# Attention of layer 0: runs of nine scores over seven one-bank PSUM tiles in place of runs of seven over tiles of three, two and two banks

## Chip, core and metric

The kernel runs on one core of a Trainium2 chip. The metric is the device time of one launch in microseconds (us). TensorE (PE) multiplies matrices into PSUM, which has eight banks of 512 float32 values on each of 128 partitions; ScalarE (ACT) computes exponentials and copies, VectorE (DVE) adds, GpSimd (POOL) and SyncE (SP) issue DMAs. Each engine works through its own queue in order and waits on semaphores for the others.

## The reference

Two layers on a tensor `x` of shape (2, 256, 64, 64), each of them `x + layer(groupnorm(x))`. Only layer 0 is touched by the change:

```python
qkv = jnp.einsum('bchw,oc->bohw', x, qkv_w) + qkv_b[None, :, None, None]
qkv = qkv.reshape(b, 3, num_heads, head_dim, n)        # 8 heads of 32, n = 4096
q, k, v = (qkv[:, 0], qkv[:, 1], qkv[:, 2])
attn_logits = jnp.einsum('bhci,bhcj->bhij', q, k) * scale
attn_weights = jax.nn.softmax(attn_logits, axis=-1)
out = jnp.einsum('bhij,bhcj->bhci', attn_weights, v)
```

So for each of 2 x 8 heads a 4096 x 4096 matrix of scores is made, its exponentials are multiplied by `v`, and the result is divided by the sums of the exponentials. Layer 1 (local attention in blocks, 1x1 convolutions and a depthwise convolution) follows for each of the two batch entries.

## The kernel before

The program does, for each of the two batch entries in turn, the projections of layer 0, `attention0`, and layer 1. `attention0` cuts the work of one entry into 16 groups `g` (8 heads, two halves of the queries), each group into 32 blocks `j` of 128 keys (`NJ`), and each block into 4 units `u` of 512 queries (`T`). A unit is a 128 x 512 tile of scores; an entry has 2048 units, the program 4096.

A unit goes through these steps:

- **Score** (L505, in `scores`): one matmul of 128 x 512 into one PSUM bank.
- **Exponential** (L511): ACT reads the scores from PSUM and writes the values to SBUF, into a ring of 28 places of 512 columns (`RING`; 17 places lie in the tile `es`, the other 11 in the tile that the profile names `v`).
- **Value product** (`quarters`, L521): four matmuls of 32 columns each, one per unit of the block, side by side on TensorE, into the bank `av`. Blocks 1 to 30 of a group are done in two halves of 256 columns (`work_of` yields between them), blocks 0 and 31 in one piece of 512. One `next(work)` is one such step, 62 for a group.
- **Sums**: for most blocks DVE adds the values of the block to running sums `e` (L558, `add_rows`); for the blocks in `SUMMED` POOL issues DMAs that add in memory to `acc` (L566, L568, `add_in_memory`).

At the end of a group ACT copies the product out (L762), the sums are multiplied by a matrix of ones into a spare PSUM bank (`sum_rows`, the same L521), and ACT copies these (L598, `finish`).

The order on PE, ACT and DVE is the order in which the program is written (`manual_schedule`). The loop at the end of `attention0` alternates two parts, which together are called a pass below: `scores` puts out up to seven scores with their exponentials, and then steps of earlier units are taken from `steps()`. `scores` uses three PSUM tiles: `sa` of three banks, `sb` and `sc` of two; one exponential reads a whole tile. `have` is the number of units that were scored before this pass, so the value products lie behind the seven scores just issued. Steps are taken while fewer than `share` are done, while the ring needs places (`must`), in the last pass, or while a bank is asked for:

```python
while begun < ready and (taken < share or begun < must or final or use is not None):
```

When something wants a PSUM bank (`wanted`: the sums of a group, a few statistics), `scores` leaves the third bank of `sa` unused in that pass, hands it out, and the pass has six scores. PSUM is full: 3 + 2 + 2 banks for scores, one for `av`.

Of the kernel before, what the change touches and what calls it, by code (L numbers as in the profile page):

```python
# [9 lines left out]
F32 = mybir.dt.float32  # L10
I32 = mybir.dt.int32
F32R = mybir.dt.float32r
AF = mybir.ActivationFunctionType
# [4 lines left out]
P = 128  # L18
B, C, H, W = 2, 256, 64, 64
N = H * W  # L20
T = 512
# [4 lines left out]
NH0 = C // HD0  # L26
# [14 lines left out]
def direct_layers(ctx: ExitStack, tc: tile.TileContext, a: dict, out: bass.AP, bad: bass.AP):  # L41
# [3 lines left out]
    nc = tc.nc  # L45
# [11 lines left out]
    psum = {}  # L57

    def w4(shape, name, dtype=F32):
        return work.tile(shape, dtype, tag="w4", name=name)  # L60
# [304 lines left out]
    SC0 = 1.0 / math.sqrt(HD0)  # L365
# [8 lines left out]
    NJ = N // P  # L374
# [77 lines left out]
    RING, RING_A = 28, 17  # L452
# [11 lines left out]
    def attention0(b, xts, held):  # L464
# [10 lines left out]
        n_units = NH0 * 2 * NJ * 4  # L475
# [4 lines left out]
        places = []  # L480
        n_places = 0

        def at_places(first, n):

            while n > 0:
                at = first % RING
                m = min(n, (RING_A if at < RING_A else RING) - at)
                yield m, es[:, at : at + m, :] if at < RING_A else held["es"][:, at - RING_A : at - RING_A + m, :]
                first, n = first + m, n - m

        def scores(spare):

            nonlocal n_places
            bank = None
            for tag, size in (("sa", 3), ("sb", 2), ("sc", 2)):
                first = len(places)
                n = min(size - (spare and size == 3), n_units - first)
                if n <= 0:
                    break
                sc = psum["sc"].tile([P, size, T], F32, tag=tag, name=f"{tag}_{b}_{first}")  # L500
                if spare and size == 3:
                    bank = sc[:, size - 1, :]
                for i in range(n):
                    g, (j, u) = (first + i) // (4 * NJ), divmod((first + i) % (4 * NJ), 4)
                    nc.tensor.matmul(  # L505
                        sc[:, i, :], held["k", g // 2][:, j * P : (j + 1) * P], held["q", g, u // 2][:, u % 2, :],
                        start=True, stop=True,
                    )
                i = 0
                for m, dst in at_places(n_places, n):  # L510
                    nc.scalar.activation(dst, sc[:, i : i + m, :], AF.Exp, scale=SC0)  # L511
                    i += m
                places.extend(range(n_places, n_places + n))
                n_places += size
            return bank

        def quarters(dst, lhs, rhs, start, stop, part=None):

# [17 lines left out]
        def add_rows(g, j):  # L536
            if j == 0:
                sums[g] = psum["sc"].tile([P, T], F32, tag="av", name=f"av_{b}_{g}")
                added[g] = [w4([P, 2, T], f"e_{b}_{g}_{w}") for w in range(2)]
                return  # L540
            for w in range(2):
                dst = added[g][w]
                if j in summed(g):
                    if w == 0:
                        add_in_memory(g, j)
                    continue
                if j == 1:
                    first = two_units(g, 0, w), two_units(g, 1, w)
                    if len(first[0]) == len(first[1]) == 1:
                        nc.vector.tensor_add(dst, first[0][0][1], first[1][0][1])  # L550
                    else:
                        for s in range(2):
                            nc.vector.tensor_add(dst[:, s, :], unit(g, 0, 2 * w + s), unit(g, 1, 2 * w + s))
                    continue
                for s, src in two_units(g, j, w):
                    if g == last and j in SUMMED_LAST:
                        continue
                    nc.vector.tensor_add(dst[:, s, :], dst[:, s, :], src)  # L558
# [11 lines left out]
        def work_of(g, j):  # L570


            if (g, j) < (last, NJ - 3):
                add_rows(g, j)
            for part in (None,) if j in (0, NJ - 1) else range(2):
                if part == 1:
                    yield
                quarters(
                    sums[g], held["v"][:, (g // 2) % 2, j, :], lambda u: unit(g, j, u), j == 0, j == NJ - 1, part
                )  # L580

        def sum_rows(g, rows):
            if g == last:
                for part in range(2):
                    for j in SUMMED_LAST:
                        quarters(rows, ones, lambda u: unit(g, j, u), j == SUMMED_LAST[0], False, part)
                    quarters(rows, ones, lambda u: acc[u], False, False, part)
                    quarters(rows, ones, lambda u: added[g][u // 2][:, u % 2, :], False, True, part)
                return
            quarters(rows, ones, lambda u: added[g][u // 2][:, u % 2, :], True, True)  # L590
# [140 lines left out]
        def steps():  # L731

            for done in range(NH0 * 2 * NJ):
                g, j = divmod(done, NJ)
                if (g, j) == (last, NJ - 3):
                    assert len(places) == n_units
                    held["rows"] = psum["sc"].tile([P, 3, T], F32, tag="sa", name=f"rows_{b}")[:, 2, :]
                    for i in (NJ - 3, NJ - 2, NJ - 1):
                        add_rows(g, i)
                    sum_rows(g, held["rows"])  # L740
                for _ in work_of(g, j):
                    yield done
                if g and j == 0:

                    for w in range(2):
                        dst = added[g - 1][w]
                        for s in range(2) if w == 0 else (slice(0, 2),):
                            nc.vector.tensor_add(dst[:, s, :], dst[:, s, :], acc[s] if w == 0 else pair)
                    waiting.clear()
                if g and j == 1:  # L750
                    wanted.append(late[0].send)
                if g and j in (9, 17):
                    next(late[0])
                for what in also.get((g, j), ()):
                    what()
                if j == 4 and g % 2 == 0 and g // 2 + 1 < NH0:
                    fetch_head(b, g // 2 + 1, held)
                if j == NJ - 1:
                    waiting.append(g)
                    avs = w4([P, 2, T], f"avs_{b}_{g}")  # L760
                    if g < last:
                        nc.scalar.copy(avs[:, 0, :], sums[g])  # L762
                    copied[g] = avs
                    late[:] = [finish(g)]
                    next(late[0])
                    if g + 2 < NH0 * 2:
                        fetch_queries(b, g + 2, held)
                yield done + 1

        E = mybir.EngineType  # L770
        with tc.manual_schedule(engines={E.PE, E.Activation, E.DVE}):

            per_group = 2 * NJ - 2
            work, begun, taken = steps(), 0, 0
            scores(False)
            final = False
            while not final:
                have = len(places)  # L780
                use = wanted.pop(0) if wanted else None
                bank = scores(use is not None)
                final = have == n_units
                ready = have // 4
                share = have * per_group // (4 * NJ) - 2

                must = sum(place < n_places + 7 - RING for place in places[: 4 * ready : 4])
                if must % NJ == 1:
                    must += 1
                assert must <= ready  # L790
                here = 0
                while begun < ready and (taken < share or begun < must or final or use is not None):
                    if use is not None and here == 2:
                        use(bank)
                        use = None
                        continue
                    here += 1
                    group = begun // NJ
                    begun = next(work)
                    taken += 1  # L800
                    if begun // NJ > group and begun >= must and not final and use is None:
                        break
                if use is not None:
                    use(bank)
            assert next(work, None) is None
            return *finish_last(last), st
# [585 lines left out]
    for b in range(B):  # L1392
        xts = x_first if b == 0 else ahead["xts"]
        w0 = w0_first if b == 0 else ahead["w0"]
        with tc.tile_pool(name=f"ps0_{b}", bufs=8, space=PSUM) as psum["ps"]:
# [7 lines left out]
            held = project0(b, xn, w0)  # L1403
# [571 lines left out]
```

## Time and profile before

| what | us |
|---|---|
| three timed runs | 3116.66, 3120.94, 3121.48 |
| median of them | 3120.94 |
| profiled execution, first to last instruction (its span) | 3116.4 |
| attention of the first entry, first score to last product | 118.4 to 1161.1 |
| attention of the second entry | 1666.3 to 2709.4 |
| the rest (projections, layer 1, weights) | about 1030 |

Of the profiled execution only the span is given; the shortest timed run is 0.3 us longer than it, the median 4.5 us. A row of the profile's groups reads: line, engine, operation, what is written <- what is read, shapes, number of instructions | time in which at least one of them ran (us), mean duration of one (ns) | idle time of the engine before them (us) and whose work ended it. Durations of neighbours on one engine overlap, so the rate of an engine is read from the distance of two starts, not from a duration. PEld is TensorE's loading of weights, which runs beside its products.

### The profile page before, as it was taken

To read this page: it belongs to the slowest core of one execution; us is meant where nothing else is said; L and a number is where in the kernel's file an instruction comes from. 1 tells how busy PE (TensorE), PEld (TensorE's weight loads), DVE (VectorE), ACT (ScalarE), POOL (GpSimd) and SP (SyncE) were. 2 spreads that over 40 slices of the span, in tenths; PEclk is the share of its full clock that TensorE was granted. 3 is DMA by queue.
4 is the path that set the end of the run, shared out by engine and by line. 5 is a ranking of instruction groups with operands and counts; after the bars stand their busy time and mean duration, and the time that the engine had idled before them with its cause. 6 is when DMAs were issued, how large, how long until landed. Compare 5 with 4: busy or idle time off the path is not lost. (4 is left out here: it accounts for less than half of the span.)

```text
span 3116.4 us, 62659 instructions
## 1 busy us (share of the span) xinstructions
PE 3031.2 (97%) x25129; PEld 1830.6 (59%) x25129; DVE 2467.0 (79%) x3126; ACT 2313.6 (74%) x2436; POOL 836.7 (27%) x923
## 2 busy tenths in 40 slices
PE   6999999999999999999989999999999999999998
PEld 4555555555555556677755555555555555476765
DVE  4599989999899999856556998989989999834543
ACT  2699999999999984622237999999999999734333
POOL 2022222222222231055301222222222222305440
PEclk9999999999999999999999999999999999999999
DMA  7969679797897761230159687796888975700000
GB/s 241 270 132 185 143 150 172 154 178 150 164 181 154 145 133 33 75 134 29 41 193 268 128 176 151 156 176 138 177 162 164 181 153 123 170 4 4 21 14 22
DMA packets 243787, 424.41 MB, mean 136 GB/s; under 512 B 99112, under 2 KB 109916, under 8 KB 241308
## 3 DMA queue, kind: packets, MB, share of 16 engines
q0 software_dynamic: 94992, 238.36, 39.8%
q1 hardware_dynamic: 147580, 181.68, 21.6%
q8 instruction: 199, 3.26, 0.4%
q14 instruction: 104, 0.85, 0.1%
q10 hardware_dynamic: 912, 0.27, 0.0%
HBM read 119.03 MB, written 68.39 MB: 60 GB/s over the span
## 5 line engine op out<-in xcount | busy, mean ns | idle before, releaser
L558 DVE TENSOR_TENSOR e<-e,es 128x1024 f32<-128x1024 f32 (+1 forms) x956 | 1038.6, 1142 | 79.6 <-ACT es L511 77.9
L521 PE MATMUL av<-es,v 128*32 128x256 f32 (+1 forms) x9644 | 746.7, 390 | 0.0
L558 DVE TENSOR_TENSOR e<-e,v 128x1024 f32<-128x1024 f32 (+1 forms) x640 | 675.2, 1107 | 47.7 <-ACT v L511 46.6
L511 ACT ACTIVATE es<-sa 128x1536 f32<-128x1536 f32 (+1 forms) x444 | 635.7, 1432 | 93.1 <-PE sa L505 54.9
L505 PE MATMUL sa<-q,k 128*128 128x512 f32 x1736 | 561.4, 430 | 9.2 <-ACT avs L598 3.5
L521 PE MATMUL av<-v 128*32 128x256 f32 (+1 forms) x6228 | 506.5, 389 | 0.0
L521 PEld LDWEIGHTS av<-es,v 128*32 128x32 f32 x9644 | 316.1, 109 | 299.4 <-issue 160.6
L505 PEld LDWEIGHTS sa<-q,k 128*128 128x128 f32 x1736 | 280.0, 188 | 291.8 <-issue 135.4
L505 PE MATMUL sc<-q,k 128*128 128x512 f32 x1180 | 371.4, 396 | 1.7 <-ACT es L511 0.7
L505 PE MATMUL sb<-q,k 128*128 128x512 f32 x1180 | 371.0, 395 | 1.1 <-ACT es L511 1.1
L521 PEld LDWEIGHTS av<-v 128*32 128x32 f32 x6228 | 216.5, 109 | 178.6 <-issue 81.2
L511 ACT ACTIVATE es<-sc 128x1024 f32<-128x1024 f32 x296 | 306.9, 1037 | 0.0
L511 ACT ACTIVATE v<-sc 128x1024 f32<-128x1024 f32 x294 | 304.9, 1037 | 0.1
L511 ACT ACTIVATE es<-sb 128x1024 f32<-128x1024 f32 x296 | 302.0, 1020 | 3.8 <-DMA acc<-es 3.8
L511 ACT ACTIVATE v<-sb 128x1024 f32<-128x1024 f32 x294 | 300.0, 1020 | 0.0
L505 PEld LDWEIGHTS sb<-q,k 128*128 128x128 f32 x1180 | 221.2, 188 | 55.4 <-ACT es L511 2.9
L505 PEld LDWEIGHTS sc<-q,k 128*128 128x128 f32 x1180 | 210.5, 188 | 71.8 <-ACT es L511 12.1
L511 ACT ACTIVATE v<-sa 128x1536 f32<-128x1536 f32 (+1 forms) x146 | 209.2, 1433 | 35.6 <-PE sa L505 17.0
L948 PE MATMUL mm<-v,wf 128*128 128x256 f32 x1024 | 227.6, 380 | 1.5 <-DVE z L957 1.5
L568 POOL DMA_DIRECT2D es<-es x116 | 98.9, 853 | 475.6 <-ACT es L511 424.3
L948 PEld LDWEIGHTS mm<-v,wf 128*128 128x128 f32 x1024 | 193.3, 190 | 36.8 <-issue 9.9
L938 POOL TENSOR_TENSOR v<-col 128x512 f32<-128x512 f32 x128 | 165.1, 1316 | 179.2 <-ACT rk_sr L1089 39.2
(262 smaller groups left out, 3179.0 us busy)
## 6 DMA issues: line engine op xcount, KB each, us to landing
acc<-es POOLq DMA_DIRECT2D x128, 512.0 KB, 6.2
acc<-v POOLq DMA_DIRECT2D x84, 512.0 KB, 6.4
es<-es POOLq DMA_DIRECT2D x136, 256.0 KB, 4.5
v<-es POOLq DMA_DIRECT2D x132, 256.0 KB, 5.1
k<-wk_halves SPq DMA_DIRECT2D x64, 512.0 KB
q<-wq_halves SPq DMA_DIRECT2D x256, 128.0 KB
v<-v POOLq DMA_DIRECT2D x90, 256.0 KB, 5.4
es<-v POOLq DMA_DIRECT2D x86, 256.0 KB, 3.9
```

The lines of the kernel that those rows point to most:

```text
L505: nc.tensor.matmul(sc[:, i, :], held["k", g // 2][:, j * P : (j + 1) * P], held["q", g, u // 2][:, u % 2, :], start=True, stop=True,)
L511: nc.scalar.activation(dst, sc[:, i : i + m, :], AF.Exp, scale=SC0)
L521: nc.tensor.matmul(dst[HD0 * u : HD0 * u + HD0, n], lhs, rhs(u)[:, n], start=start, stop=stop)
L558: nc.vector.tensor_add(dst[:, s, :], dst[:, s, :], src)
L568: nc.gpsimd.dma_start(out=dst, in_=src, accum_op=ALU.add)
L938: (nc.gpsimd.tensor_add if plus else nc.gpsimd.tensor_sub)(dst, rows(one), rows(two))
L948: nc.tensor.matmul(mm[:, m, r, :], wf[:, k, 4 * r + q, m * P : (m + 1) * P], v[r // 2][:, r % 2, k, :], start=k == 0, stop=k == KC - 1,)
```

## The change

It replaces the three score tiles by seven tiles of one bank, `s0` to `s6`, which are used in rotation (`next_bank`), each unit with its own exponential. A run has nine scores (`PHASE`) instead of seven, so the eighth and ninth score of a run use the banks of its first and second. Value products are taken up to `behind` = 7 units behind the units scored so far, this run included. A bank that is asked for is the next in the rotation after the run, and the run keeps its nine scores. The condition for taking steps gains `ending` (the last two steps of a group), and the last three blocks are left for the last pass.

```diff
-        def scores(spare):
+        BANKS, PHASE = 7, 9
+
+        def next_bank():
 
             nonlocal n_places
-            bank = None
-            for tag, size in (("sa", 3), ("sb", 2), ("sc", 2)):
-                first = len(places)
-                n = min(size - (spare and size == 3), n_units - first)
-                if n <= 0:
-                    break
-                sc = psum["sc"].tile([P, size, T], F32, tag=tag, name=f"{tag}_{b}_{first}")
-                if spare and size == 3:
-                    bank = sc[:, size - 1, :]
-                for i in range(n):
-                    g, (j, u) = (first + i) // (4 * NJ), divmod((first + i) % (4 * NJ), 4)
-                    nc.tensor.matmul(
-                        sc[:, i, :], held["k", g // 2][:, j * P : (j + 1) * P], held["q", g, u // 2][:, u % 2, :],
-                        start=True, stop=True,
-                    )
-                i = 0
-                for m, dst in at_places(n_places, n):
-                    nc.scalar.activation(dst, sc[:, i : i + m, :], AF.Exp, scale=SC0)
-                    i += m
-                places.extend(range(n_places, n_places + n))
-                n_places += size
-            return bank
+            at = n_places
+            n_places += 1
+            return at, psum["sc"].tile([P, T], F32, tag=f"s{at % BANKS}", name=f"s_{b}_{at}")
+
+        def scores():
+
+            for unit in range(len(places), min(len(places) + PHASE, n_units)):
+                g, (j, u) = unit // (4 * NJ), divmod(unit % (4 * NJ), 4)
+                at, sc = next_bank()
+                nc.tensor.matmul(
+                    sc, held["k", g // 2][:, j * P : (j + 1) * P], held["q", g, u // 2][:, u % 2, :],
+                    start=True, stop=True,
+                )
+                ((_, dst),) = at_places(at, 1)
+                nc.scalar.activation(dst[:, 0, :], sc, AF.Exp, scale=SC0)
+                places.append(at)
...
-                    held["rows"] = psum["sc"].tile([P, 3, T], F32, tag="sa", name=f"rows_{b}")[:, 2, :]
+                    held["rows"] = next_bank()[1]
...
+            behind, reach = 7, PHASE + 1
             work, begun, taken = steps(), 0, 0
-            scores(False)
-            final = False
-            while not final:
-                have = len(places)
+            while begun < NH0 * 2 * NJ:
+                scores()
                 use = wanted.pop(0) if wanted else None
-                bank = scores(use is not None)
-                final = have == n_units
-                ready = have // 4
+                bank = next_bank()[1] if use is not None else None
+                final = len(places) == n_units
+                have = n_units if final else len(places) - behind
+                ready = max(0, have) // 4
                 share = have * per_group // (4 * NJ) - 2
 
-                must = sum(place < n_places + 7 - RING for place in places[: 4 * ready : 4])
+                must = sum(place < n_places + reach - RING for place in places[: 4 * ready : 4])
...
-                while begun < ready and (taken < share or begun < must or final or use is not None):
+                while begun < ready:
                     if use is not None and here == 2:
                         use(bank)
                         use = None
                         continue
+                    ending = taken % per_group >= per_group - 2
+                    if not (taken < share or ending or begun < must or final or use is not None):
+                        break
+                    if not final and begun == NH0 * 2 * NJ - 3:
+                        break
```

## The prediction

> **What bounds the kernel now.** The change touches only the attention stretches, so I first ask the busy time of the engines in the first of them (118 to 1164 us of the span), then the order of time on TensorE inside it, then that on ScalarE.
>
> ```profile
> core 0: us, PE busy (x) PEld busy (x) DVE busy (x) ACT busy (x) POOL busy (x), PEclk, DMA share, GB/s
> 118.00:1164.00 1046.00, 1039.25 (x10192) 591.28 (x10192) 958.29 (x980) 974.80 (x926) 279.27 (x340) 1.00 0.80 161
> ```
>
> PE is busy in 99%, but ACT (93%) and DVE (92%) are not far behind, and the clock is fully granted. A PE that is never idle can still lose time between products of different kinds, which only the starts show. The timeline of PE over one pass (start, duration, instructions):
>
> ```profile
> 606.18 0.96 PE L505 MATMUL sa<-q,k 128*128 128x512 f32 x3
> 606.98 0.63 PE L505 MATMUL sb<-q,k 128*128 128x512 f32 x2
> 607.45 0.63 PE L505 MATMUL sc<-q,k 128*128 128x512 f32 x2
> 608.00 1.50 PE L521 MATMUL av<-es,v 128*32 128x256 f32 x24
> 609.43 0.96 PE L505 MATMUL sa<-q,k 128*128 128x512 f32 x3
> ```
>
> From start to start the pass takes 3.25 us: 1.82 for seven scores, 1.43 for 24 records of products (8 records are one step of 256 columns). Inside a run two scores start 0.231 us apart, inside the products 8 records take 0.432 (0.054 each). At that rate the pass would take 7 x 0.231 + 3 x 0.432 = 2.91. The rest, 0.337, is paid at the changes of kind: the second score starts 0.337 after the first (0.106 too late), the first product 0.326 after the last score (0.095 too late), and the products' 1.432 hold 0.136 more than 3 x 0.432. The starts of all 588 runs in the trace (294 passes an entry) give the same numbers: medians 0.337, 0.231 and 0.327.
>
> So the two attention stretches can be added up from PE alone: 588 runs x 0.337 = 198; 4096 scores x 0.231 = 946; 15872 records at 0.054, those of blocks 0 and 31 doubled, = 885; the sums of 30 groups, 0.864 each, = 26. Together 2055, and the passes add up to 23 more (5.6 of them at the two starts). PE sets the pace nearly everywhere, and 198 us of its time are changes of kind. Now ACT, its timeline over the end of a group, and, in a second fence, rows of its groups by shape:
>
> ```profile
> 639.64 1.01 ACT L511 ACTIVATE es<-sb 128x1024 f32<-128x1024 f32 x1
> 640.54 1.03 ACT L511 ACTIVATE es<-sc 128x1024 f32<-128x1024 f32 x1
> 641.44 0.61 ACT L762 COPY avs<-av 128x512 f32<-128x512 f32 x1
> 641.92 1.49 ACT L511 ACTIVATE es<-sa 128x1536 f32<-128x1536 f32 x1
> 643.27 1.05 ACT L511 ACTIVATE es<-sb 128x1024 f32<-128x1024 f32 x1
> ```
>
> ```profile
> L1132 ACT ACTIVATE y<-py 128x512 f32<-128x512 f32 x32 | 19.1, 597 | 49.6 <-PE py L1128 48.1 <-PE at_lr L1058 1.5
> L762 ACT COPY avs<-av 128x512 f32<-128x512 f32 x30 | 18.2, 606 | 0.0
> L598 ACT COPY avs<-sa 128x512 f32<-128x512 f32 x30 | 17.6, 586 | 0.1
> ```
>
> Starts lie closer than durations: 0.90 us after a 1024-wide exponential (median 0.901), 1.35 after a 1536-wide one (1.349), 0.46 to 0.48 after the 512-wide copy (0.463 where no later wait shows). Seven units cost ACT 1.349 + 0.901 + 0.904 = 3.15 us, under the pass's 3.25 to 3.69.
>
> **The change, part by part.**
>
> *Fewer runs on PE.* In the order of instructions of the changed kernel the runs of scores are 454 in place of 588; the number of scores and of value products is the same. 134 x 0.337 = 45.1 us less. That is all on the path, since PE sets the pace. A pass that hands out a bank no longer shrinks to six scores, which is in this count.
>
> *An exponential per bank.* 1770 exponentials become 4096 of 512 columns. No row shows a 512-wide exponential behind another, so its price p, from start to start, is bounded by neighbours. Lower end: a line through 1.349 and 0.901 gives 0.453. Higher: a `sa` of two banks (in passes that hand out the third) is 0.922 from start to start, one of three 1.349, so a bank of 512 columns costs 0.427 and the first exponential of a pass has 0.069 fixed. An `sb`, next in the stream, keeps 0.901 - 0.854 = 0.047, say 0.048. The copy keeps 0.463 - 0.427 = 0.036, and it is 0.011 shorter than an activation of its size (586 against 597). With 0.048, p = 0.475; with 0.069, 0.496. I take 0.475, the price of a stream of activations, and keep 0.453 to 0.496.
>
> [...]
>
> ACT's need at my price: 4096 x 0.475 = 1946, and 60 copies x 0.463 = 28, together 1974. PE's is 2055 - 45 = 2010. ACT has 36 us of slack, 1.1 us for each of 32 groups, where today it has 2055 - (588 passes x 3.15 + 28) = 175. This is the narrow place of the change. Every ns on p is 4.1 us of ACT; the two needs meet at p = 0.484, and ACT alone takes the 2078 of today at p = 0.500. With the waits on both sides I put the point of no gain at 0.492 to 0.496.
>
> *New waits in the run.* Each score waits for the exponential that read its bank seven scores earlier, the eighth and ninth for the first two of their own run. Behind them on PE are all the products. When PE leaves a run, at most seven exponentials are open, 3.3 us of ACT, and products of four steps with the changes of kind take 2.2. So at the next run up to 1.1 us are open, the first new exponential ends at about 1.7 (0.6 more), and the eighth score is due at 1.72, the ninth at 1.95 against 2.2 for its bank. A pass of four steps (9 x 0.231 + 0.337 + 1.728 = 4.14) is shorter than nine exponentials (4.28), one of five (4.58) longer; the order of the changed kernel goes 4, 5, 4, 4, 5, the mean with the groups' ends 2010 / 454 = 4.43. The late ninth score costs at most 0.13 in half of the runs, 30 us, and nothing where the five-step pass has paid ahead; banks hold 1.1 us of lead, so I take 5 us, ends 0 and 30. The products themselves wait for nothing new: the ninth score has waited for the exponential seven behind, the last that they read.
>
> *The ends of groups.* The copies L762 and L598 stand behind the open exponentials as today. The sums now wait for the exponential that read the third bank of the run, long done after two steps. Today's 17 us of stalls outside the starts, mostly 0.3 to 0.4 at such places, stay; with less ACT slack they could be 0 to 10 us more, which I put into the 30 above.
>
> *Sums, DMAs, ring.* DVE's adds are 1336 of 1024 columns against 1332, and 232 against 236 halves: nothing. Its 958 us busy (durations, whose neighbours overlap by 0.08) fit into 1046 - 22 = 1024 with 94%. It runs behind ACT and holds ring places only; ACT shows no wait for it now. The queues of POOL and SP have the same DMAs in the same order but for pairs split at the ring's edge; ACT waits for them 2.3 us an entry now, and a place comes round after 28 x 0.49 = 13.8 us in place of 14.1, while they land in 4 to 6.4. Nothing, with 5 us as the other end.
>
> *Sum.* -45.1 + 5 = -40. The span of 3116.4 becomes 3076; the median of the timed runs lies 4.5 over that span, so 3120.9 - 40 = 3081.
>
> **Rivals.**
>
> ACT eats part of it: p between 0.485 and 0.492. Then ACT is the bound in the four-step passes, and -25 to -5 remain: 3096 to 3116. For it speaks how close the two needs are, 36 us in 2010; against it the 0.048 that no size of stream exceeds.
>
> ACT becomes the bound, and the kernel is slower: p over 0.496, which decides the sign. The mechanism is one: 2326 more activations, each with its own fixed part and its own wait for PE and for DVE or a DMA, whose order ACT has to take one at a time. From 0.500 on each 10 ns cost some 37 us: 0.510 gives 3185. For it: only the copy shows such a width in a stream, and a fixed part after a wait is 0.069, reached if ACT, now often just ahead of PE, starts cold each time. Against it: an ACT that waits has time to spare, so cold starts fall where they cost little.
>
> The change does not speed anything, because DVE, at 94%, becomes late with ring places and PE falls back to today's pace: about 3120. For it: the groups near the end have 5 us of statistics more. Against it: ACT waits for DVE nowhere now.
>
> **How the numbers follow.** Forecast -40: 0.66. Partial gain: 0.10, of which 0.07 over the bound. Slower by ACT: 0.19. DVE: 0.05, half of it no change and half slower. A measurement of this kernel can tell 0.2%, 6.2 us, from no change. Faster: 0.66 + 0.07 = 0.73; same: 0.03 + 0.025 = 0.055, taken as 0.06; slower: 0.21. The forecast's own range is 3070 (p = 0.453, no new stall, and today's stalls shortened by 6) to 3098 (p at 0.482 or stalls of 20). For 8 in 10 the upper end takes in the partial gain and the slower side up to p = 0.496, 15 us over today: 3136. Left out are p of 0.5 and more, about 0.16, and 0.03 below.
>
> **What would show it.** In the profile after: 454 runs of nine, each change of kind still 0.337 in sum; PE at 99% of an attention of about 1023 us an entry; exponentials of 512 columns 0.47 to 0.48 from start to start where none waits; ACT about 97% busy. Wrong are these steps if scores wait for ACT by more than 30 us in sum, if starts are over 0.49 apart in a stream (then ACT shows no idle time and PE idles ahead of the eighth and ninth score), or if ACT waits for DVE or a DMA.

## The result: no change, 3119.6 us

Twelve timed runs of the changed kernel have a median of 3119.57 us, twelve of the kernel before on the same chip 3117.85. The ratio is 1.0001 with a 95% interval of 0.9993 to 1.0009: the gain of 40 us that was forecast is not there. The profiled execution of the changed kernel took 3119.5 us, 1.8 more than its span.

The busy time in the first attention stretch, the same view as before the change:

```profile
core 0: us, PE busy (x) PEld busy (x) DVE busy (x) ACT busy (x) POOL busy (x), PEclk, DMA share, GB/s
118.00:1164.00 1046.00, 1041.85 (x10202) 610.12 (x10200) 952.52 (x978) 1028.36 (x2090) 280.58 (x340) 1.00 0.80 162
```

PE still reads 99.6%, but ACT went from 975 us to 1028, 98%. PE's busy time can't show short waits here: a score's record lasts 0.395 us in the median and the next one starts 0.231 behind it, and in this trace no score that came less than 0.2 us late behind another one has idle time ahead of it. ScalarE's timeline over the end of a group (start, time from the first start to the last end, number of instructions in the row):

```profile
631.77 0.61 ACT L510 ACTIVATE es<-s 128x512 f32<-128x512 f32 x1
632.27 5.50 ACT L510 ACTIVATE v<-s 128x512 f32<-128x512 f32 x11
637.51 3.20 ACT L510 ACTIVATE es<-s 128x512 f32<-128x512 f32 x6
640.62 0.59 ACT L758 COPY avs<-av 128x512 f32<-128x512 f32 x1
641.11 5.56 ACT L510 ACTIVATE es<-s 128x512 f32<-128x512 f32 x11
```

Read by starts, eleven exponentials take 637.51 - 632.27 = 5.24 us, 0.476 each, the price that was forecast. Read by ends they take longer. The first row ends at 632.38, the second at 637.77: 5.39 us for eleven, 0.490 each. The third ends at 640.71: 2.94 for six, again 0.490. Over both attention stretches the distance of two neighbouring ends has the median 0.490 and lies between 0.481 (first percentile) and 0.494 (95th). Starts and ends drift apart: a stream begins with exponentials of 0.60 us, and each lasts some 13 ns longer than the one ahead, up to 0.9 and more. Where the durations fall back, the ends keep their distance: the exponential that starts at 604.61 lasts 0.812, the next starts 0.702 behind it and lasts 0.601, and ends 0.491 behind it. So a start is recorded here before the one ahead has ended (631.77 + 0.61 = 632.38 against 632.27 in the rows above), and the ends give the pace of the work. So the page's mean duration is no price either:

```profile
L510 ACT ACTIVATE es<-s 128x512 f32<-128x512 f32 x2500 | 1264.0, 730 | 8.3 <-PE s L505 7.1
L510 ACT ACTIVATE v<-s 128x512 f32<-128x512 f32 x1596 | 824.3, 737 | 10.7 <-PE s L505 7.1
```

From first to last exponential the two entries take 2069 us by ends. 4096 exponentials and the copies between them at 0.490 are 2037 of it, and only 33 us are gaps (places where the next end comes over 20 ns late). ScalarE is the bound.

What PE pays for it shows in its loading of weights, over two runs of nine:

```profile
604.78 1.91 PEld L505 LDWEIGHTS s<-q,k 128*128 128x128 f32 x9 [0.41 <-ACT es L510]
607.04 1.45 PEld L517 LDWEIGHTS av<-es,v 128*32 128x32 f32 x32 [0.35 <-issue]
608.90 1.68 PEld L505 LDWEIGHTS s<-q,k 128*128 128x128 f32 x8 [0.41 <-ACT v L510]
610.87 0.19 PEld L505 LDWEIGHTS s<-q,k 128*128 128x128 f32 x1 [0.28 <-ACT es L510]
611.29 0.11 PEld L517 LDWEIGHTS av<-es,v 128*32 128x32 f32 x2 [0.24 <-issue]
```

In the first run all nine weights load in a row and the products begin 2.26 us after the first load. In the second the ninth load waits for an exponential and the products begin after 2.39. The wait for the bank stands on the weight load (4086 of the 4096 loads of scores carry one), and a held load starts 0.05 us after the exponential has ended (median 0.052 in the 143 runs whose ninth score is over 20 ns late). A load that is in time starts 0.22 us ahead of its score, beside the score ahead; a late one starts with its score (0.002 us ahead), and then the first product follows that score by 0.431 us instead of 0.326. So a bank that is free when its score is due is too late here: the load of the last score was held in 258 of 450 runs, the score itself was late in only 143, and in the other 115 the first product still came 0.432 us after it.

Summed as in the prediction, the passes are 66 us longer than their rates, against 23 before; this sum is called PE's excess below. Of the 66, late eighth and ninth scores are 27 and products that come late behind a held load 25. 454 runs in place of 588 save 45, the added waits take 43.

### The profile page after: what moved, and what is told of

It is laid out like the page before. It is cut to its first block, busy times and chain, and to the rows that moved or that the text cites. A ratio compares the mean times of both kernels' runs of the same rounds, so it can differ in the third digit from the quotient of the medians.

```text
span 3117.7 us, 65724 instructions
## 1 busy us (share of the span) xinstructions
PE 3037.0 (97%) x25129; PEld 1867.5 (60%) x25129; DVE 2457.3 (79%) x3122; ACT 2420.4 (78%) x4762; POOL 838.3 (27%) x923
## 5 line engine op out<-in xcount | busy, mean ns | idle before, releaser
L510 ACT ACTIVATE es<-s 128x512 f32<-128x512 f32 x2500 | 1264.0, 730 | 8.3 <-PE s L505 7.1
L505 PE MATMUL s<-q,k 128*128 128x512 f32 x4096 | 1126.5, 413 | 7.0 <-ACT v L510 3.6
L505 PEld LDWEIGHTS s<-q,k 128*128 128x128 f32 x4096 | 732.8, 188 | 436.8 <-ACT es L510 186.7
L510 ACT ACTIVATE v<-s 128x512 f32<-128x512 f32 x1596 | 824.3, 737 | 10.7 <-PE s L505 7.1
L564 POOL DMA_DIRECT2D acc<-es x118 | 116.2, 995 | 114.8 <-ACT es L510 64.5
L564 POOL DMA_DIRECT2D es<-v x72 | 61.3, 852 | 310.0 <-ACT v L510 308.3
L955 DVE TENSOR_TENSOR z<-z,mm 128x512 f32<-128x512 f32 x32 | 22.0, 687 | 139.0 <-ACT z L954 138.6
L564 POOL DMA_DIRECT2D v<-es x112 | 124.4, 1111 | 18.0 <-ACT es L510 13.6
L564 POOL DMA_DIRECT2D acc<-v x78 | 75.2, 964 | 67.8 <-ACT es L510 30.7
L564 POOL DMA_DIRECT2D v<-v x78 | 85.9, 1101 | 12.3 <-ACT v L510 7.5
```

The costliest lines, as they stand in the source:

```text
L505: nc.tensor.matmul(sc, held["k", g // 2][:, j * P : (j + 1) * P], held["q", g, u // 2][:, u % 2, :], start=True, stop=True,)
L510: nc.scalar.activation(dst[:, 0, :], sc, AF.Exp, scale=SC0)
L564: nc.gpsimd.dma_start(out=dst, in_=src, accum_op=ALU.add)
L955: nc.vector.tensor_add(z[:, 0], z[:, 1], mm[:, :, 0, :])
```

## Experiments

Theory A: the change moved the bound to ScalarE, since an exponential has a fixed part of 0.063 us (0.490 less 0.427 for its 512 columns, the cost of one more bank in the kernel before, which is 0.834 ns a column and 0.833 in an expectation below) whatever its width, and 2326 more of them cost what PE saves. Theory B: what costs is the reuse of two banks within a run, whatever ScalarE's rate. All ratios are to the kernel before, run on the same chip.

**Runs of eight.**

```diff
-        BANKS, PHASE = 7, 9
+        BANKS, PHASE = 7, 8
```

> The changed kernel with runs of eight scores in place of nine (510 runs instead of 454), all else as changed. Theory A, ScalarE is the bound: in the changed kernel's trace exponentials of 512 columns end 0.490 us apart, so ScalarE needs 4096 x 0.490 = 2007 us and 29 more for the copies, 2036 in all, whatever the length of a run; PE needs 2010 + 56 x 0.337 = 2029. So the time stays within 10 us of the changed kernel, 3110 to 3120, and exponentials still end 0.490 apart. Theory B, the reuse of two banks inside one run is what costs (waits of the eighth and ninth score and their weight loads, about 50 us): of these more than half go, 19 us of changes of kind come back, so some 25 us are gained, 3092 to 3098.

Measured 3100.32 us, 0.9942 (0.9928 to 0.9955): faster than both kernels. Exponentials still end 0.490 apart, and ScalarE's gaps fall from 33 to 15 us; PE's excess falls from 66 to 29. The gain of 17 us lies between the two expectations. ScalarE's need of 2037 is a floor that all three lengths of run share; how near a kernel comes to it depends on the gaps, which A had left out. In the changed kernel 32 of the 33 us lie in or right behind passes of five and more steps of products; with runs of eight 13 of the 15 are waits of the copies at the ends of groups.

**Runs of seven, an exponential per bank alone.**

```diff
-        BANKS, PHASE = 7, 9
+        BANKS, PHASE = 7, 7
```

> The changed kernel with runs of seven: one exponential per bank alone, no longer runs (584 of them, no bank used twice in a run). Theory A: PE needs 2010 + 130 x 0.337 = 2054 and ScalarE 2036, so PE is the bound again by a little: within 8 us of the kernel before, 3112 to 3126, scores wait for banks under 15 us in sum. Theory B: the same time as before, without any wait for a bank. Theory C, the separate wait of every score holds up its weight load and costs PE about 0.1 us at many scores, whatever the run: clearly slower, 3145 or more.

Measured 3101.70, 0.9951 (0.9937 to 0.9965). All three expectations miss it. With nearly the old number of runs (584 against 588) it is 16 us faster than before, because PE's excess falls from 23 to 7. C is refuted: with a wait at each score PE's excess is 7 us in all 584 runs together. Of the 23 us before, 8 lay in the passes that lend a bank, 6 at the two starts and 10 in others (rounded); with runs of seven 2, 3 and 2 are left of them. Whether the gain comes from banks that are released and lent one by one or from the new order of the loop, which came with them, was not separated.

**Exponentials of 448 columns in the changed kernel.**

```diff
-                nc.scalar.activation(dst[:, 0, :], sc, AF.Exp, scale=SC0)
+                cols = T if at < RING else T - 64
+                nc.scalar.activation(dst[:, 0, :cols], sc[:, :cols], AF.Exp, scale=SC0)
```

> The changed kernel with exponentials of 448 columns instead of 512 once the ring has been filled (an eighth of the exponentials is left out, stale values stand in their place); every score, product, sum, wait and order stays. Theory A: exponentials end 0.437 apart, ScalarE needs 1790 + 29 us, PE with 2010 is the bound, and the gain that was forecast appears: 30 to 42 us, 3076 to 3090; waits of scores fall below 20 us in sum. Theory B: banks are still reused inside a run and the waits mostly stay, at most 10 us gained, 3108 or more.

Measured 3064.20, 0.9832 (0.9819 to 0.9846), 53 us less. The window of the first entry's attention:

```profile
core 0: us, PE busy (x) PEld busy (x) DVE busy (x) ACT busy (x) POOL busy (x), PEclk, DMA share, GB/s
118.00:1136.00 1018.00, 1016.48 (x10192) 609.33 (x10194) 947.61 (x975) 937.35 (x2085) 276.99 (x338) 1.00 0.82 166
```

ACT is at 92%, its exponentials end 0.437 apart, PE's excess is 14 us. Scores, runs and banks are those of the changed kernel; only ScalarE's time per bank was cut. B, "whatever ScalarE's rate", is refuted: with the same reuse of banks the gain is there, larger than A said (30 to 42): 45 us of changes of kind and 9 of the excess that stood there before (23 to 14).

**The same cut in the kernel before.**

```diff
-                    nc.scalar.activation(dst, sc[:, i : i + m, :], AF.Exp, scale=SC0)
+                    cols = T if n_places < RING else T - 64
+                    nc.scalar.activation(dst[:, :, :cols], sc[:, i : i + m, :cols], AF.Exp, scale=SC0)
```

> The kernel before with each exponential reading 448 of each bank's 512 columns once the ring has been filled (the same eighth left out). Theory A: there PE sets the pace (2055 us of need against 1868 for ScalarE), so nothing is gained but part of the 17 us of stalls: 3105 to 3120. If ScalarE was already near the bound before, 30 us or more are gained.

Measured 3109.66, 0.9974 (0.9965 to 0.9983): 8 us, the fall of PE's excess from 23 to 15. Before the change ScalarE was not the bound; the same cut is worth 8 us there and 53 after it.

**Exponentials at the forecast price.** As the cut above, with `T - 18`.

> The changed kernel with exponentials of 494 columns in place of 512 once the ring is filled (18 columns in 512 left out), which by theory A end 0.063 + 494 x 0.833 ns = 0.475 us apart: the price that the prediction gave to a full one. Theory A: then the rest of the prediction's sum should hold and the time lie 30 to 45 us under the kernel before, 3073 to 3088. If the wrong price was not the only step that failed (waits in the run undervalued as well), 3089 to 3105.

Measured 3088.38, 0.9903 (0.9888 to 0.9917). They end 0.475 apart in the median, as worked out; two rows of ScalarE's timeline, whose ends (637.06 and 640.37) give 3.31 us for seven:

```profile
631.51 5.55 ACT L511 ACTIVATE es<-s 128x494 f32<-128x494 f32 x11
636.93 3.44 ACT L511 ACTIVATE v<-s 128x494 f32<-128x494 f32 x7
```

The 30 us lie at the edge between the two expectations: at its own price the forecast of 40 is three quarters there, and most of the rest is PE's excess, which is 35 us where the prediction had 23 + 5. Of the 35, 7.7 lie in two passes, one an entry, in which ScalarE waits 2.4 and 2.6 us for a late sum on VectorE.

**The copies at the ends of groups moved to VectorE,** with runs of eight and of nine.

```diff
-                        nc.scalar.copy(avs[:, 0, :], sums[g])
+                        nc.vector.tensor_copy(avs[:, 0, :], sums[g])
...
-            nc.scalar.copy(avs[:, 1, :], rows)
+            nc.vector.tensor_copy(avs[:, 1, :], rows)
```

> Runs of eight, and the two 512-column copies at the end of a group (the product out of av, the sums out of the spare bank) done by VectorE instead of ScalarE; nothing left out. Theory A (ScalarE's rate of 0.490 an exponential is the bound): its need falls by 60 x 0.48 = 29 us, from 2037 to 2008, under PE's 2029, so 10 to 20 us are gained on runs of eight: 3082 to 3092. Theory B (reuse of banks inside a run costs, whatever ScalarE's load): within 4 us of runs of eight, 3097 to 3104. If VectorE (92% busy) comes late with the copies, slower than runs of eight.

> The changed kernel, runs of nine, with the same two copies on VectorE; nothing left out. Theory A: ScalarE needs 2008, PE 2010; 15 to 29 us less than the changed kernel, 3090 to 3104. Theory B: as the changed kernel, 3115 to 3121.

Measured 3108.59, 0.9967 (0.9958 to 0.9977), and 3123.79, 1.0021 (1.0012 to 1.0030): both slower than without the move (0.9942 and 1.0001). Waits of the first entry with runs of eight (engine, line, waited for: us in total, times, longest):

```profile
DVE avs L594 <- PE s L517: 19.9, 15, 1.8
DVE avs L758 <- PE av L517: 18.7, 12, 1.6
PE av L517 <- DVE avs L758: 4.3, 3, 3.1
```

VectorE, which was busy for 949 of 1038 us with runs of eight, now stands still at the copies until PE has ended the group (38.6 us by the first two rows), and three times PE waits up to 3.1 us for `av`. ScalarE's gaps rise from 15 to 52 us, more than the 29 that it was spared: by these sums the copies had stood largely where it had nothing else to do, though no run moved one of the two copies alone. A's expectation had counted them as if they lay in its stream.

**Two banks per exponential where the rotation allows.** One tile of seven banks, used in the same rotation; the main part of the edit, with the pairs at (2, 3, 4, 5, 7) for runs of nine and (1, 2, 3, 4, 5, 6) for runs of eight:

```diff
+        all_banks = psum["sc"].tile([P, 7, T], F32, tag="s", name=f"s_{b}")
...
-            return at, psum["sc"].tile([P, T], F32, tag=f"s{at % BANKS}", name=f"s_{b}_{at}")
+            return at, all_banks[:, at % BANKS, :]
...
+                if held_back is not None:
+                    ((_, dst),) = at_places(held_back, 2)
+                    k = held_back % BANKS
+                    nc.scalar.activation(dst, all_banks[:, k : k + 2, :], AF.Exp, scale=SC0)
```

> The changed kernel, runs of nine, with one seven-bank tile whose banks are used in the same rotation; the first two exponentials of a run stay single (their banks are used again in the run), later neighbours are taken two banks at a time where neither the rotation nor the ring breaks: 1270 exponentials of 1024 columns and 1556 of 512. Nothing is left out. Theory A (the fixed 0.063 us of each exponential made ScalarE the bound): in the trace of before 1024-wide ones end 0.915 apart, so ScalarE needs 1270 x 0.915 + 1556 x 0.490 + 29 = 1953 us, PE with 2010 is the bound, and most of the forecast gain returns: 3075 to 3092. Theory B (the reuse of banks inside the run itself is what costs): the reuse is unchanged, so 3108 or more.

> The same with runs of eight (only the first exponential of a run has to stay single: 1496 of 1024 columns, 1104 of 512). Nothing is left out. Theory A: ScalarE needs 1939 us, PE 2029, so PE is the bound with few waits: 19 us over runs of nine by its changes of kind, less their remaining waits, 3085 to 3100. Theory B: as runs of eight with single exponentials, 3097 to 3104.

Measured 7120.53 and 7052.11, 2.2845 (2.2818 to 2.2872) and 2.2624 (2.2597 to 2.2651). They say nothing on A or B. For runs of nine, the line of TensorE's granted clock (tenths of full speed in 40 slices) and then the timeline of TensorE and ScalarE:

```profile
PEclk8666666666666666679976666666666666666799
```

```profile
1001.04 1.22 PE L509 MATMUL s<-q,k 128*128 128x512 f32 x2 [1.11 <-ACT es L517]
1002.29 1.02 ACT L517 ACTIVATE es<-s 128x1024 f32<-128x1024 f32 x1 [1.31 <-PE s L509]
1003.37 0.79 PE L509 MATMUL s<-q,k 128*128 128x512 f32 x1 [1.11 <-ACT es L517]
1004.20 0.60 ACT L528 ACTIVATE es<-s 128x512 f32<-128x512 f32 x1 [0.88 <-PE s L509]
```

Scores and exponentials alternate: the score at 1003.37 starts when the exponential just ahead has ended (1003.31), though by the rotation its bank was read by an earlier one. All banks are one tile in this kernel; that a score therefore waits for the last exponential of any bank is the author's guess, which no run shows: pairs over separate tiles were not run. The granted clock was 0.69 over the span (0.68 with runs of eight), against 0.99 in the kernel before.

The kernels with single exponentials side by side. PE's need is the prediction's sum at their number of runs; ScalarE's is the number of exponentials and the copies between them times the median distance of their ends; PE's excess is what the passes take over their rates; ScalarE's gaps are the distances of ends that are more than 20 ns over that median. All in us, both entries:

| kernel | runs | PE need | ScalarE need | PE excess | ScalarE gaps | ratio |
|---|---|---|---|---|---|---|
| changed, runs of 9 | 454 | 2010 | 2037 | 66 | 33 | 1.0001 |
| runs of 8 | 510 | 2029 | 2037 | 29 | 15 | 0.9942 |
| runs of 7 | 584 | 2054 | 2037 | 7 | 17 | 0.9951 |
| 9, copies on DVE | 454 | 2010 | 2008 | 70 | 67 | 1.0021 |
| 8, copies on DVE | 510 | 2029 | 2008 | 36 | 52 | 0.9967 |
| 9, 494 columns | 454 | 2010 | 1975 | 35 | 63 | 0.9903 |
| 9, 448 columns | 454 | 2010 | 1817 | 14 | 202 | 0.9832 |

So neither A nor B is enough by itself. ScalarE's 2037 with runs of seven, where no bank is used twice in a run, leaves an excess of 7; runs of nine with a ScalarE that has time to spare (1817) leave 14. Runs of nine at 2037 leave 66: it takes both.

## Why the prediction was wrong

The step that failed is the price p in "An exponential per bank". It was read as 0.475 from start to start, and it is 0.490 from end to end. 4096 x 15 ns = 61 us: ScalarE's need, the copies included, became 2037 us where the prediction had 1974, above PE's 2010 and not below it. The right value stood in the five lines shown there. Their ends are 640.65, 641.57, 642.05, 643.41 and 644.32; the distances 0.92, 0.48, 1.36 and 0.91 belong to exponentials of 1024, a copy of 512, exponentials of 1536 and 1024 columns. In the trace of before 1024-wide ones end 0.912 (`sb`) and 0.918 (`sc`) after the one ahead, so 0.059 to 0.065 are fixed beside 0.853, and p comes out at 0.486 to 0.492. Starts gave 0.048. In the kernel before ScalarE mostly paused ahead of an `sa` (it ends 1.47 us after the one ahead in the median, where 1.28 for three banks and 0.063 make 1.34), so the lead of starts over ends stayed small there; in a stream without a pause it grows to 0.3 us. The prediction's own sign for this step, starts 0.47 to 0.48 apart, came true (0.477), and the price was wrong all the same.

The second step is "New waits in the run", 5 us with ends 0 and 30. At the true price the excess rose by 43, from 23 to 66; at the forecast's own price (494 columns) by 12, to 35, a part of it the waits for VectorE of the next paragraph. So most of this miss follows from p. Two things were left out beside it: the wait holds the weight load, which starts 0.22 us ahead of its score when it is in time, and behind a late one the change to the products was 0.105 longer (0.431 against 0.326).

A smaller step that failed is "Sums, DMAs, ring", put at nothing. In the first entry ScalarE waits for VectorE 0.2 us by the view of waits, but in the second it waits 3.1 us for one sum that holds a place of the ring, and VectorE had stood 10.9 us waiting for a DMA (timeline of the changed kernel):

```profile
2364.09 0.69 DVE L609 TENSOR_TENSOR avs<-avs 128x512 f32<-128x512 f32 x1 [10.93 <-DMA avs<-drec]
2367.33 3.36 ACT L510 ACTIVATE v<-s 128x512 f32<-128x512 f32 x6 [3.11 <-DVE e L554]
```

This pass takes 5.3 us over its rates. The prediction had named such a wait as a sign of being wrong, and had 5 us as the other end.

The rest held. The trace has 454 runs, the second score of a run 0.337 after the first and others 0.231 apart, and with ScalarE relieved the saving is real (53 us less at 448 columns). "The two needs meet at p = 0.484" was right as arithmetic; the point of no gain, put at 0.492 to 0.496, lies at about 0.490. Some smaller figures were off: 10 ns more on p are 41 us of ScalarE by the prediction's own 4.1 a ns, not 37; the additions of 512 columns are 264 before and 256 after, not 236 and 232; and the median of twelve timed runs before is 3 us under the 3120.9 that it started from. The rival with p between 0.485 and 0.492 named the cause, with 0.10; its -25 to -5 were too much gain, since the waits came on top.

The exponentials of the runs end 0.490, 0.475 and 0.437 us apart at 512, 494 and 448 columns, which is 0.063 + 0.834 ns a column.

## What to carry to other kernels

Read the rate of an engine from the distance of ends in a stream, or from both: where durations grew along a stream here, starts ran ahead of the work (0.477 apart against 0.490). When a change splits the work of the second-busiest engine into smaller instructions, price the fixed part to a few ns first; here 15 ns an instruction, 61 us, were more than the whole forecast of 40. A ring of buffers that is shorter than a burst tied the two engines together here (PE's excess 66 us with runs of nine over seven banks, 29 with eight, 7 with seven), so shorten the burst until no buffer is used again too early (here runs of eight or seven, 0.9942 and 0.9951, not told apart), and price a late buffer with the weight load that it holds (0.105 us more to the first product here).

## What was new of the hardware

- In the trace of the changed kernel the start of an exponential was recorded up to 0.3 us ahead of the pace of its work: in a stream of 512-wide ones starts are 0.477 apart, ends 0.490, and durations grow from 0.60 to over 0.9 us.
- In the same trace a score whose bank was late started 0.053 us after the end of the exponential, its weight load with it (0.052), and the next product came 0.431 instead of 0.326 us after it.
- The kernel of runs of nine with pairs, whose TensorE stood still again and again for 0.7 to 1.1 us between scores (rows above and the same timeline), shows a granted clock of 0.69 over its span (0.99 in the kernels with single exponentials). In the trace of the changed kernel one wait of 2.4 us for a bank (until 2367.98) was followed by a granted clock of 0.56 between 2370 and 2372 us and 0.58 between 2372 and 2374, and of 1.00 in the two us before and the two after. Why the clock fell was not shown.
